# Attention rounds in another order: value products between projection and transposes, parts turned in halves, long products spread over the rounds

## The chip, the cores and the metric

The kernel runs on one core of a Trainium2 chip. The metric is the device time of one launch in microseconds (us), the median over several runs. The page and the trace come from one more launch under the hardware profiler. Engines are TensorE (PE), its weight load (PEld), VectorE (DVE), ScalarE (ACT), GpSimd (POOL) and SyncE (SP), which issues the DMAs.

## The reference

A block of four layers on `x` of 4 x 256 x 512 in fp32, each with a residual and a layer norm ahead of it. Only the first one, attention, is touched:

```python
x = x + _L0_attn_a_ref(_layernorm(x), ...)      # attention with an adapter
x = x + _L0_ffn_ref(_layernorm(x), ...)         # clustered linear layer
x = x + _L0_attn_b_ref(_layernorm(x), ...)      # state-space mixer
x = x + _L0_ffn_ref(_layernorm(x), ...)
```

Attention has 4 batches of 256 tokens, 32 heads of 16 channels, rotary embedding, a causal mask, and a second softmax over 10 adapter rows:

```python
q, k, v = split(x @ w_attn.T);  q, k = rope(q), rope(k)
y = softmax(causal(q @ k.T / sqrt(16))) @ v
y = y + gating * softmax(q @ ak.T / sqrt(512)) @ av
return y @ w_proj.T
```

## The kernel before

`attention` takes the first 370 us or so of the launch, `mixer` the rest. fp32 products against weights are made as three products of fp32r halves (`mm3`, L107 to L114): a "long" product of 128 tokens with a 512 x 512 weight is 12 matmuls of 512 columns.

Attention runs in rounds. Round `i` belongs to batch `b = i // 8` and to four heads, `u = i % 8`; there are 32 rounds and seven more for what trails behind. Each stage of the four heads runs in a round of its own:

- `scores` (L410 to L446), round `i`: 8 products of q and k parts into four `sc` buffers and 4 that add the mask (L427, L434), then on DVE a maximum (`nmx`, L439) and on ACT eight exps (L442).
- `turn` (L448 to L459), one round later: 12 transposes of `e` into three `ptr` buffers, copied to `eT` by DVE (two) and ACT (one).
- `weigh` (L461 to L479), two rounds later: 16 value products into `py`, copied to `ys` by ACT.
- `gathered` (L481 to L492), three rounds later: 2 transposes of `ys` (`try`), then 1/sum and a product on DVE into `y`.

The parts that `scores` reads, for eight heads at a time, are made by `pieces(b, q)`: of q (`f = 0`) and k (`f = 1`) and both token halves, a stack is filled (`stacked`: a cast on ACT, a subtraction on POOL, L304 and L305) and turned by four transposes (`trp`, L379). DVE copies the q parts to `pc0`, ACT the k parts to `pc1` (L381). Each `f` has two stack buffers (`NS = 2`). All 16 transposes stand at the end of every even round, for the next two.

Around these run jobs, Python generators that yield the name of the place in a round at which they go on: "long", "turn" or "values". They are `prepared(b + 1)` (norm, two q, two k and two v products of the next batch; the rotation `rotated` is three DVE products that read `pq`, L280 to L284, and a POOL addition), `adapter` (the adapter's keys and values, once), `adapted(b)` (adapter softmax, `pt` and `pya`), `closed` (adds the adapter's part, turns `y`, and makes the output projection `po`), and `fed` (one tile of 128 tokens of the next layer, `Feed`). `adapter_scores` makes one `pa` product per even round and one `tra` transpose. A job goes on at the next round's place of that name.

PE's instructions are issued exactly in the order of the Python program (`manual_schedule`); the other engines' order is set by the framework. So the order of the calls in a round is PE's order:

```python
es_[i] = scores(b, u)
step("long", i)
... adapter_scores ...
eTs[i - 1] = turn(es_.pop(i - 1))
gathered(*divmod(i - 3, 8), yss.pop(i - 3))
step("turn", i)
step("values", i)
yss[i - 2] = weigh(*divmod(i - 2, 8), eTs.pop(i - 2))
... pieces, in even rounds ...
```

PSUM is split in three pools: three buffers "m" for all products and transposes except scores (`sc`, four buffers) and values (`py`, one). A buffer is taken again when ACT or DVE has read it.

The long products fall as follows: `prepared` in rounds 1, 2, 4, 5, 6, 7 of a batch (for the later batches 9, 10, 12 to 15 and 17, 18, 20 to 23), `po` of batches 0, 1 and 2 as two at once in rounds 12, 20 and 28, `fed` tiles in rounds 29 to 34.

Of the kernel before, what the change touches and what calls it, by code (L numbers as in the profile page):

```python
# [20 lines left out]
P = 128  # L21
# [56 lines left out]
def hybrid_kernel(  # L78
# [153 lines left out]
    def attention(later):  # L232
        with ExitStack() as es:
# [84 lines left out]
            def adapter_weights():  # L318
                pk = ps.tile([80, C], F32, name="pk", tag="m")
                mm3(pk, [[v[:, k, :] for v in wt] for k in range(KC)],  # L320
                    [[v[:, k, :] for v in wk_s] for k in range(KC)])
                ak = p2.tile([80, NH, HD], F32, name="ak", tag="t1")
                bdk = col("bdk")[:20].unsqueeze(1).unsqueeze(3).to_broadcast([20, NH // 2, 2, HD])
                nc.vector.tensor_tensor(
                    ak[:20].rearrange("p (b e) d -> p b e d", e=2),
                    pk[:20].rearrange("p (b e d) -> p b e d", e=2, d=HD), bdk, ALU.mult,
                )
                for q in range(4):
                    s = stacked(ak[:20, q * 8 : q * 8 + 8, :], 1, 20)
# [26 lines left out]
            def prepared(b):  # L356

                where = (ps, "m") if b else (ps_s, "sc")
                xs = []
                for c in range(2):  # L360
                    yield "turn"
                    xs.append(normed(norm, 2 * b + c))
                    for f, w in ((0, wq_s), (1, wk_s)):
                        yield "long"
                        qk[b, c, f] = rotated(projected(xs[c], w, where), c, f, f"r{f}{c}")
                for c in range(2):
                    yield "long"
                    nc.scalar.copy(vs[b % 2][:, c, :C], projected(xs[c], wv_s, where))

            def pieces(b, q):  # L370

                out = []
                for f in range(2):
                    o = p2.tile([P, 4, L], F32R, name=f"pc{f}", tag=f"pc{f}")
                    for c in range(2):
                        s = stacked(qk[b, c, f][:, q * 8 : q * 8 + 8, :], f)
                        tr = ps.tile([P, 4, P], F32R, name="trp", tag="m")
                        for j in range(4):
                            nc.tensor.transpose(tr[:, j, :], s[:, j * P : (j + 1) * P], con)  # L379
                        cs = slice(c * P, (c + 1) * P)  # L380
                        nc.scalar.copy(o[:, :, cs], tr) if f else nc.vector.tensor_copy(o[:, :, cs], tr)  # L381
                    out.append(o)
                turned_[b, q] = out

# [28 lines left out]
            def scores(b, u):  # L413
# [18 lines left out]
                for c, pr, sc in made:  # L432
# [4 lines left out]
                    )  # L437
                    nm = p3.tile([P, 2], F32, name="nmx", tag="nmx", bufs=6)
                    nc.vector.tensor_reduce(nm, sc, AX.X, ALU.max, negate=True)  # L439
# [55 lines left out]
            def adapted(b):  # L495
# [12 lines left out]
                nc.gpsimd.tensor_tensor(sc, sc, wide(sa), ALU.mult)  # L508
                yield "turn"
                paTs = []  # L510
                for c in range(2):
# [7 lines left out]
                    nc.scalar.copy(paTs[c], pt)  # L519
                yield "values"  # L520
                for c in range(2):
# [8 lines left out]
            def closed(b, ks):  # L530

                st = state[b]
                for k in ks:
                    y = st["y"][:, :, k * P : (k + 1) * P]
                    nc.vector.tensor_tensor(y, y, st["ya"][:, :, k * P : (k + 1) * P], ALU.add)
                yield "turn"
                for k in ks:
# [5 lines left out]
                if 3 not in ks:  # L543
                    return
                yield "long"
                st = state.pop(b)
                pos = []
                for c in range(2):
                    pos.append(ps.tile([P, C], F32, name="po", tag="m"))
                    cs = slice(c * P, (c + 1) * P)  # L550
                    mm3(pos[c], [[v[:, k, cs] for v in st["yT"]] for k in range(KC)],
                        [[v[:, k, :] for v in wp_s] for k in range(KC)])
                for c, po in enumerate(pos):
                    t = 2 * b + c
                    ins = nc.vector.tensor_tensor(x[:, t, :], x[:, t, :], po, ALU.add)
                    if t == TT - 1:
                        tc.keep_in_program_order(ins)
                    if feed is None:
                        continue
                    feed.norm.stats(t)  # L560
                    feed.norm.root(t, t + 1)
                    if b < B - 1:
                        slow.append(fed(feed, t))
                    else:
                        late[t] = p2.tile([P, C], F32, name="axn", tag="t1")
                        feed.norm.scale(t, late[t])
                for t, xn in late.items():
# [3 lines left out]
                    late[t] = xs  # L571

            def fed(f, t):
                yield "turn"
                xs = normed(f.norm, t)
                yield "long"
                f.tile(t, xs, [ps.tile([P, FH], F32, name="pd", tag="m") for _ in range(2)])
# [32 lines left out]
            def adapter():  # L610
                split(wt, wte_s)
                yield "long"
                adapter_weights()
                yield "long"
                asides.append(adapter_scores(0, 0))
                next(asides[-1])
                adapter_values()
# [3 lines left out]
            feed, late = None, {}  # L621
            asides, at = [], {}

            def begun(j):
                at[j] = next(j, None)
                if at[j]:
                    jobs.append(j)

            def step(stage, i):

                for j in [j for j in jobs if at[j] == stage and moved.get(j) != i]:
                    moved[j] = i
                    at[j] = next(j, None)
                    if at[j] is None:
                        jobs.remove(j)

            moved = {}
            begin(0)
            pieces(0, 0)
            with tc.manual_schedule(engines={nc.tensor.engine}):  # L640
                for i in range(n + 7):
                    b, u = divmod(i, 8)
                    if i < n:
                        if i == 0:
                            begun(adapter())
                        if u == 0:
                            if i:
                                begin(b)
                            if b + 1 < B:
                                begun(prepared(b + 1))  # L650
                        es_[i] = scores(b, u)
                    if i == n - 6:
                        inner.close()
# [8 lines left out]
                        slow += [fed(feed, t) for t in range(4)]  # L662
                    if slow and i >= n - 4:
                        begun(slow.pop(0))
                    step("long", i)
                    if i < n and u % 2 == 0 and i > 0:
                        asides.append(adapter_scores(b, u // 2))
                        next(asides[-1])
                    if 1 <= i <= n:
                        eTs[i - 1] = turn(es_.pop(i - 1))  # L670
# [572 lines left out]
```

## Time and profile before

| | us |
|---|---|
| median of 3 runs | 1904.89 (1898.11 to 1905.41) |
| profiled execution | 1901.88 |
| its span | 1900.1 |
| attention rounds 0 to 30 | 294.98, PE busy 260.75 |
| one exp of 256 columns, ACT | 0.47 |
| four `nmx`, DVE | 1.95 |
| rotation, three DVE products | 0.69, 0.41, 0.41 |
| `eT`, `pc` copy, DVE / ACT | 0.68 / 0.59 |
| stack cast ACT, subtraction POOL | 0.41, 0.46 |

A row of stretches, as shown below, gives the length, then for each engine its busy time and, in brackets, the number of its instructions. A line of waits names the waiting engine, tile and line, what it waited for, and the total, the number and the longest in us. In a timeline a row is start, duration, engine, line and operation; in brackets the idle time ahead of it and what ended it. PE's ends are modelled, so small overlaps are normal.

### The profile page before, as it was taken

The numbers are of one execution on the slowest core, as the hardware profiler recorded it, in microseconds if no ns is written. First come the engines' busy times: TensorE is split into PE (matmuls) and PEld (weight loads), VectorE is DVE, ScalarE is ACT, GpSimd is POOL, SyncE is SP. The second block draws the span as 40 slices with busy tenths as digits, with TensorE's granted clock in tenths as the row PEclk, the third lists the DMA queues.
The fourth block names the chain that finished last, engine by engine and source line by source line (L and its number), as shares of the span: only waits on it lengthen the run. The fifth ranks groups of instructions, "written<-read, shape, count | busy, mean of one in ns | idle before, by whom it ended". The sixth has DMA issues, their size and how long they took to land.

```text
span 1900.1 us, 29893 instructions
## 1 busy us (share of the span) xinstructions
PE 1817.5 (96%) x10690; PEld 1452.2 (76%) x10690; DVE 1477.0 (78%) x2324; ACT 1381.4 (73%) x2873; POOL 350.2 (18%) x308
## 2 busy tenths in 40 slices
PE   7988889889999999999999999999999999999997
PEld 5766667777777887878788788777787888787786
DVE  5666667778998778777977797778778877877777
ACT  5676686468898767867877787678777876786753
POOL 5221110011221221121212122211211121122100
PEclk8999999989999999999999999999999999999999
DMA  4000000025555544554544454545454544455341
GB/s 142 1 1 1 22 14 1 23 65 172 172 183 183 155 162 147 159 168 148 167 160 156 145 183 139 173 143 171 151 172 141 159 156 165 144 161 166 112 124 49
DMA packets 151909, 240.35 MB, mean 126 GB/s; under 512 B 12368, under 2 KB 77520, under 8 KB 151760
## 3 DMA queue, kind: packets, MB, share of 16 engines
q1 hardware_dynamic: 151760, 238.44, 39.1%
q8 instruction: 84, 1.38, 0.3%
q14 instruction: 65, 0.53, 0.1%
HBM read 202.75 MB, written 35.65 MB: 125 GB/s over the span
## 4 chain that ended last, share of the span: by engine, by line
PE 77%; DVE 9%; ACT 8%; DMA 2%; issue 2%; POOL 1%; SPq 0%; DVEq 0%; ACTq 0%; POOLq 0%
PE pp L112 12%; PE pp L113 12%; PE pp L114 11%; PE pyy L961 8%; PE pog L112 6%; PE pog L114 6%; PE pog L113 6%; PE trx L946 3%; ACT e L442 3%; DVE acc L887 2%; DMA wor<-in_wout_dram 1%; PE ptr L457 1%; PE sc L427 1%; DVE nmx L439 1%; PE py L467 1%
## 5 line engine op out<-in xcount | busy, mean ns | idle before, releaser
L112 PE MATMUL pp<-mx,w 128*128 128x512 f32 (+1 forms) x1160 | 465.4, 401 | 7.9 <-DVE acc L887 7.4
L113 PE MATMUL pp<-mx,w 128*128 128x512 f32 (+1 forms) x1160 | 454.1, 391 | 0.0
L114 PE MATMUL pp<-mx,w 128*128 128x512 f32 (+1 forms) x1160 | 453.8, 391 | 0.0
L887 DVE SCALAR_TENSOR_TENSOR acc<-pp,cw_s,acc 128x1012 f32<-128x1012 f32 (+2 forms) x240 | 304.9, 1270 | 23.2 <-ACT acc L880 22.6
L935 DVE TENSOR_TENSOR em<-em,gm 128x1536 f32<-128x1536 f32 x128 | 228.2, 1783 | 93.9 <-ACT em L929 85.4
L112 PEld LDWEIGHTS pp<-mx,w 128*128 128x128 f32 x1160 | 218.5, 188 | 65.6 <-issue 10.2
L114 PEld LDWEIGHTS pp<-mx,w 128*128 128x128 f32 x1160 | 218.5, 188 | 45.6 <-issue 0.4
L113 PEld LDWEIGHTS pp<-mx,w 128*128 128x128 f32 x1160 | 218.7, 189 | 40.7 <-issue 0.7
L984 POOL TENSOR_TENSOR sq<-sq,acc 128x1024 f32<-128x1024 f32 x55 | 132.6, 2411 | 577.4 <-ACT acc L983 577.4
L923 POOL TENSOR_SCALAR_AFFINE_SELECT r<-r 128x512 f32<-128x512 f32 x128 | 133.7, 1045 | 542.8 <-DMA r<-cumd 441.2
L104 ACT CAST w<-wr 128x512 fp32r<-128x512 f32 x144 | 88.5, 615 | 188.7 <-PE pp L113 165.8
L112 PE MATMUL pog<-wo,gh 128*128 128x512 f32 x512 | 204.6, 400 | 0.0
L928 ACT ACTIVATE em<-r,col_t 128x128 f32<-128x128 f32 x512 | 165.0, 391 | 48.8 <-PE pyy L961 47.0
L113 PE MATMUL pog<-wo,gh 128*128 128x512 f32 x512 | 200.1, 391 | 0.0
L114 PE MATMUL pog<-wo,gh 128*128 128x512 f32 x512 | 199.9, 391 | 0.0
L961 PE MATMUL pyy<-em,xd 128*64 128x256 f32 (+1 forms) x2048 | 189.1, 329 | 3.1 <-DVE em L935 3.1
L961 PEld LDWEIGHTS pyy<-em,xd 128*64 128x64 f32 x2048 | 133.9, 137 | 64.6 <-issue 21.4
L931 ACT ACTIVATE em<-r,col_t 128x128 f32<-128x128 f32 x512 | 166.5, 388 | 0.0
L919 DVE TENSOR_SCALAR em<-r,col_t 128x128 f32<-128x128 f32 x512 | 137.3, 327 | 12.3 <-PE pyy L961 10.1
L947 DVE TENSOR_TENSOR xd<-trx,dt_t 128x512 f32<-128x512 f32 x128 | 86.2, 683 | 54.4 <-PE trx L946 54.3
L105 DVE TENSOR_TENSOR w<-wr,w 128x512 fp32r<-128x512 f32 x139 | 97.9, 705 | 38.1 <-ACT w L104 38.1
L442 ACT ACTIVATE e<-sc,nmx 128x256 f32<-128x256 f32 (+1 forms) x256 | 103.7, 431 | 24.9 <-DVE nmx L439 24.9
(287 smaller groups left out, 3180.4 us busy)
## 6 DMA issues: line engine op xcount, KB each, us to landing
wr<-in_win_dram SPq DMA_DIRECT2D x287, 256.0 KB, 2.8
r<-cumd SPq DMA_DIRECT2D x128, 512.0 KB, 4.1
spill<-gb SPq DMA_DIRECT2D x63, 512.0 KB, 2.8
gr<-spill SPq DMA_DIRECT2D x120, 256.0 KB, 3.4
wor<-in_wout_dram SPq DMA_DIRECT2D x64, 256.0 KB, 3.1
out_dram<-x SPq DMA_DIRECT2D x8, 256.0 KB, 2.3
x<-in_x_dram SPq DMA_DIRECT2D x1, 1536.0 KB, 10.3
gr<-spill SPq DMA_DIRECT2D x8, 192.0 KB, 2.6
```

The lines of the kernel that those rows point to most:

```text
L112: nc.tensor.matmul(o, lh, rh, start=(first and k == 0), stop=False)
L113: nc.tensor.matmul(o, lh, rl, start=False, stop=False)
L114: nc.tensor.matmul(o, ll, rh, start=False, stop=(last and k == n - 1))
L442: nc.scalar.activation(es_[c][:, 2 * j + pr, :], sc[:, j, :], AF.Exp, bias=nm[:, j : j + 1], accum_out=rs[:, c, h : h + 1],)
L887: nc.vector.scalar_tensor_tensor(av[:, :, d:], pv[:, :, : L - d], cw_s[:, ch, tap : tap + 1], av[:, :, d:], ALU.mult, ALU.add,)
L919: nc.vector.tensor_scalar(e[:, b, 2, :], rv[:, b, 1, :], col_t[:, h, b, 1:2], 0.0, ALU.subtract, ALU.min,)
L923: nc.gpsimd.affine_select(rv[:, :, 0, :], rv[:, :, 0, :], pattern=[[0, B], [1, P]], compare_op=ALU.is_ge, fill=-1e30, base=0, channel_mult ...
L928: nc.scalar.activation(e[:, b, 1, :], rv[:, b, 1, :], AF.Exp, bias=col_t[:, h, b, 2:3])
L931: nc.scalar.activation(e[:, b, 0, :], rv[:, b, 0, :], AF.Exp, bias=col_t[:, h, b, 0:1])
L935: nc.vector.tensor_tensor(e, e, gm, ALU.mult)
L961: nc.tensor.matmul(py[d, b, k * P :], xd[:, 2 * b + k, d], es2[hh][:, b, 2 * k : 2 if k == 0 else 3, :].rearrange("p s i -> p (s i)"), sta ...
L984: (nc.gpsimd if n < NB - 1 else nc.vector).tensor_tensor(sq, sq, x2, ALU.add)
```

## The change

Within a round, `weigh` and the "values" place now come after the long products and the parts, and ahead of `turn` and `gathered`. `pieces` is now a generator for one `f`: its first half fills two stacks at the end of a round, its second half turns them in the next round, behind the long product; q parts in even rounds, k parts in odd ones. Jobs yield a place and the earliest round, `FEEDS` names the rounds that start a `Feed` tile, and `begun` and `jobs` become `moved` and `nexts`. `closed` makes its two projections in two rounds (14 and 15, 22 and 23, 28 and 29); only the last batch makes both at once. `prepared` has its long products in rounds 2 to 7, 9 to 14 and 17 to 22. The adapter's keys are made at the "turn" place of round 1, its values and first scores in round 2. `Feed` is opened at round 24 instead of 26. `nmx` has four buffers, not six. The loop has one empty round less.

```diff
+                return ak
+
+            def adapter_keys(ak):
                 for q in range(4):
                     s = stacked(ak[:20, q * 8 : q * 8 + 8, :], 1, 20)
...
                 where = (ps, "m") if b else (ps_s, "sc")
+                r = 8 * (b - 1)
                 xs = []
+
+                def made(c, f):
+                    w = wk_s if f else wq_s
+                    qk[b, c, f] = rotated(projected(xs[c], w, where), c, f, f"r{f}{c}")
+
+                yield "turn", r
+                xs.append(normed(norm, 2 * b))
+                yield "long", r + 1
+                made(0, 0)
+                yield "turn", r + 1
+                xs.append(normed(norm, 2 * b + 1))
+                yield "long", r + 2
+                made(0, 1)
+                yield "long", r + 3
+                made(1, 0)
+                yield "long", r + 4
+                made(1, 1)
                 for c in range(2):
-                    yield "turn"
-                    xs.append(normed(norm, 2 * b + c))
-                    for f, w in ((0, wq_s), (1, wk_s)):
-                        yield "long"
-                        qk[b, c, f] = rotated(projected(xs[c], w, where), c, f, f"r{f}{c}")
+                    yield "long", r + 5 + c
+                    nc.scalar.copy(vs[b % 2][:, c, :C], projected(xs[c], wv_s, where))
+
+            def pieces(b, q, f):
+
+                st = [stacked(qk[b, c, f][:, q * 8 : q * 8 + 8, :], f) for c in range(2)]
+                yield
+                o = p2.tile([P, 4, L], F32R, name=f"pc{f}", tag=f"pc{f}")
                 for c in range(2):
-                    yield "long"
-                    nc.scalar.copy(vs[b % 2][:, c, :C], projected(xs[c], wv_s, where))
-
-            def pieces(b, q):
-
-                out = []
-                for f in range(2):
-                    o = p2.tile([P, 4, L], F32R, name=f"pc{f}", tag=f"pc{f}")
-                    for c in range(2):
-                        s = stacked(qk[b, c, f][:, q * 8 : q * 8 + 8, :], f)
-                        tr = ps.tile([P, 4, P], F32R, name="trp", tag="m")
-                        for j in range(4):
-                            nc.tensor.transpose(tr[:, j, :], s[:, j * P : (j + 1) * P], con)
-                        cs = slice(c * P, (c + 1) * P)
-                        nc.scalar.copy(o[:, :, cs], tr) if f else nc.vector.tensor_copy(o[:, :, cs], tr)
-                    out.append(o)
-                turned_[b, q] = out
+                    tr = ps.tile([P, 4, P], F32R, name="trp", tag="m")
+                    for j in range(4):
+                        nc.tensor.transpose(tr[:, j, :], st[c][:, j * P : (j + 1) * P], con)
+                    cs = slice(c * P, (c + 1) * P)
+                    nc.scalar.copy(o[:, :, cs], tr) if f else nc.vector.tensor_copy(o[:, :, cs], tr)
+                turned_.setdefault((b, q), []).append(o)
+                yield
...
-                    nm = p3.tile([P, 2], F32, name="nmx", tag="nmx", bufs=6)
+                    nm = p3.tile([P, 2], F32, name="nmx", tag="nmx", bufs=4)
...
-                yield "turn"
+                yield "turn", 8 * b + 8
...
-                yield "values"
+                yield "values", 8 * b + 9
...
-                yield "long"
                 st = state.pop(b)
                 pos = []
                 for c in range(2):
+                    if c == 0 or b < B - 1:
+                        yield "long", 8 * b + {B - 1: 0, B - 2: 12}.get(b, 14) + c
                     pos.append(ps.tile([P, C], F32, name="po", tag="m"))
                     cs = slice(c * P, (c + 1) * P)
                     mm3(pos[c], [[v[:, k, cs] for v in st["yT"]] for k in range(KC)],
                         [[v[:, k, :] for v in wp_s] for k in range(KC)])
+                    if b < B - 1:
+                        finished(b, c, pos[c])
+                if b < B - 1:
+                    return
                 for c, po in enumerate(pos):
-                    t = 2 * b + c
-                    ins = nc.vector.tensor_tensor(x[:, t, :], x[:, t, :], po, ALU.add)
-                    if t == TT - 1:
-                        tc.keep_in_program_order(ins)
-                    if feed is None:
-                        continue
-                    feed.norm.stats(t)
-                    feed.norm.root(t, t + 1)
-                    if b < B - 1:
-                        slow.append(fed(feed, t))
-                    else:
-                        late[t] = p2.tile([P, C], F32, name="axn", tag="t1")
-                        feed.norm.scale(t, late[t])
+                    finished(b, c, po)
                 for t, xn in late.items():
                     tr = ps.tile([P, KC, P], F32, name="tr", tag="m")
                     xs = [p2.tile([P, KC, P], F32R, name=f"axs{j}", tag=f"axs{j}") for j in range(2)]
                     feed.norm.turn(xn, tr, xs)
                     late[t] = xs
...
+            def finished(b, c, po):
+                t = 2 * b + c
...
+                feed.norm.stats(t)
+                feed.norm.root(t, t + 1)
+                if b < B - 1:
+                    slow.append(fed(feed, t))
+                else:
+                    late[t] = p2.tile([P, C], F32, name="axn", tag="t1")
+                    feed.norm.scale(t, late[t])
+
             def fed(f, t):
-                yield "turn"
+                yield "turn", 0
                 xs = normed(f.norm, t)
-                yield "long"
+                yield "long", 0
                 f.tile(t, xs, [ps.tile([P, FH], F32, name="pd", tag="m") for _ in range(2)])
...
             def adapter():
                 split(wt, wte_s)
-                yield "long"
-                adapter_weights()
-                yield "long"
+                yield "long", 0
+                ak = adapter_weights()
+                yield "turn", 0
+                adapter_keys(ak)
+                yield "long", 2
                 asides.append(adapter_scores(0, 0))
                 next(asides[-1])
                 adapter_values()
...
+            asides, nexts = [], {}
+            FEEDS = (25, 26, 27, 29, 31, 32)
+
+            def moved(j, i):
+
+                v = next(j, None)
+                if v is None:
+                    nexts.pop(j, None)
+                else:
+                    nexts[j] = v[0], v[1] if v[1] else i + 1
 
             def step(stage, i):
 
-                for j in [j for j in jobs if at[j] == stage and moved.get(j) != i]:
-                    moved[j] = i
-                    at[j] = next(j, None)
-                    if at[j] is None:
-                        jobs.remove(j)
-
-            moved = {}
+                for j in [j for j, (s, r) in nexts.items() if s == stage and r <= i]:
+                    moved(j, i)
...
             begin(0)
-            pieces(0, 0)
+            for f in range(2):
+                for _ in pieces(0, 0, f):
+                    pass
+            part = pieces(0, 1, 0)
+            next(part)
+            moved(adapter(), -1)
             with tc.manual_schedule(engines={nc.tensor.engine}):
-                for i in range(n + 7):
+                for i in range(n + 6):
                     b, u = divmod(i, 8)
                     if i < n:
-                        if i == 0:
-                            begun(adapter())
                         if u == 0:
                             if i:
                                 begin(b)
                             if b + 1 < B:
-                                begun(prepared(b + 1))
+                                moved(prepared(b + 1), i)
                         es_[i] = scores(b, u)
-                    if i == n - 6:
+                    if i == n - 8:
                         inner.close()
                         feed = Feed("f", *(
...
-                    if slow and i >= n - 4:
-                        begun(slow.pop(0))
+                    if i in FEEDS:
+                        moved(slow.pop(0), i - 1)
                     step("long", i)
+                    if part:
+                        next(part)
+                    part = None
                     if i < n and u % 2 == 0 and i > 0:
                         asides.append(adapter_scores(b, u // 2))
                         next(asides[-1])
+                    step("values", i)
+                    if 2 <= i <= n + 1:
+                        yss[i - 2] = weigh(*divmod(i - 2, 8), eTs.pop(i - 2))
                     if 1 <= i <= n:
                         eTs[i - 1] = turn(es_.pop(i - 1))
...
                     if i < n and u == 7:
-                        begun(adapted(b))
-                    step("values", i)
-                    if 2 <= i <= n + 1:
-                        yss[i - 2] = weigh(*divmod(i - 2, 8), eTs.pop(i - 2))
+                        moved(adapted(b), i)
                     if 3 <= i < n + 3:
                         if (i - 3) % 8 == 6:
-                            begun(closed((i - 3) // 8, (0, 1, 2)))
+                            moved(closed((i - 3) // 8, (0, 1, 2)), i)
                         if (i - 3) % 8 == 7:
-                            begun(closed((i - 3) // 8, (3,)))
-                    if i < n and u % 2 == 0:
-                        if u < 6:
-                            pieces(b, u // 2 + 1)
-                        elif b + 1 < B:
-                            pieces(b + 1, 0)
-                assert not jobs and not slow
+                            moved(closed((i - 3) // 8, (3,)), i)
+
+                    b, u = divmod(i + 3, 8)
+                    if b < B and i < n:
+                        part = pieces(b, u // 2, (i + 1) % 2)
+                        next(part)
+                assert not nexts and not slow
```

More of the change, by code (lines that the diff above doesn't have):

```diff
@@ L571, in closed @@
                     late[t] = xs
+            def finished(b, c, po):
+                t = 2 * b + c
+                ins = nc.vector.tensor_tensor(x[:, t, :], x[:, t, :], po, ALU.add)
+                if t == TT - 1:
+                    tc.keep_in_program_order(ins)
+                if feed is None:
+                    return
+                feed.norm.stats(t)
[5 more added lines that the diff above has]
+                    feed.norm.scale(t, late[t])
             def fed(f, t):
-                yield "turn"
+                yield "turn", 0
                 xs = normed(f.norm, t)
-                yield "long"
+                yield "long", 0
                 f.tile(t, xs, [ps.tile([P, FH], F32, name="pd", tag="m") for _ in range(2)])
@@ L611, in adapter @@
                 split(wt, wte_s)
-                yield "long"
-                adapter_weights()
-                yield "long"
+                yield "long", 0
+                ak = adapter_weights()
+                yield "turn", 0
+                adapter_keys(ak)
+                yield "long", 2
                 asides.append(adapter_scores(0, 0))
@@ L621, in attention @@
             feed, late = None, {}
-            asides, at = [], {}
-            def begun(j):
-                at[j] = next(j, None)
-                if at[j]:
-                    jobs.append(j)
-            def step(stage, i):
-                for j in [j for j in jobs if at[j] == stage and moved.get(j) != i]:
-                    moved[j] = i
-                    at[j] = next(j, None)
-                    if at[j] is None:
-                        jobs.remove(j)
-            moved = {}
-            begin(0)
-            pieces(0, 0)
+            asides, nexts = [], {}
[6 more added lines that the diff above has]
+                    nexts[j] = v[0], v[1] if v[1] else i + 1
+            def step(stage, i):
+                for j in [j for j, (s, r) in nexts.items() if s == stage and r <= i]:
+                    moved(j, i)
+            begin(0)
+            for f in range(2):
[4 more added lines that the diff above has]
+            moved(adapter(), -1)
             with tc.manual_schedule(engines={nc.tensor.engine}):
-                for i in range(n + 7):
+                for i in range(n + 6):
                     b, u = divmod(i, 8)
                     if i < n:
-                        if i == 0:
-                            begun(adapter())
                         if u == 0:
```

## The prediction

> **What bounds the kernel now.** I read the page first. TensorE (PE) is busy nearly throughout and the chain that ended last is mostly PE's:
>
> ```profile
> span 1900.1 us, 29893 instructions
> PE 1817.5 (96%) x10690; PEld 1452.2 (76%) x10690; DVE 1477.0 (78%) x2324; ACT 1381.4 (73%) x2873; POOL 350.2 (18%) x308
> ...
> PE 77%; DVE 9%; ACT 8%; DMA 2%; issue 2%; POOL 1%; SPq 0%; DVEq 0%; ACTq 0%; POOLq 0%
> ```
>
> So the number of PE instructions, which the change leaves alone, sets the floor; only PE's idle time in attention, and its clock there, can be won. I cut the trace at the first score product of each attention round, 35.79 to 330.77 us for rounds 0 to 30. The columns are length, then busy time with the instruction count of PE, PEld, DVE, ACT and POOL, then granted clock, DMA share and GB/s:
>
> ```profile
> 129.40:139.89 10.49, 9.76 (x86) 7.79 (x83) 8.68 (x20) 7.05 (x27) 1.72 (x3) 1.00 0.00 1
> 139.89:147.46 7.57, 5.62 (x49) 3.63 (x49) 5.04 (x12) 6.03 (x23) 1.35 (x4) 0.88 0.01 2
> 147.46:163.22 15.76, 15.28 (x104) 12.16 (x100) 9.18 (x19) 6.54 (x25) 2.03 (x3) 0.95 0.00 0
> 163.22:170.39 7.17, 6.51 (x56) 5.00 (x55) 4.94 (x12) 4.58 (x21) 1.88 (x3) 1.00 0.01 2
> ...
> sum 294.98, PE 260.75 PEld 202.57 DVE 189.04 ACT 204.77 POOL 50.67; mean PE 8.41 PEld 6.53 DVE 6.10 ACT 6.61 POOL 1.63
> ```
>
> PE idles 294.98 - 260.75 = 34.2 us in these rounds. Round 11 has no long product: 1.95 us idle and a clock of 0.88; round 12 has three and idles 0.48. The waits of PE in attention say what ends the idle time:
>
> ```profile
> PE try L484 <- DVE eT L458: 6.0, 9, 1.0
> PE ptr L457 <- DVE t L284: 4.0, 6, 0.7
> PE ptr L457 <- DVE eT L458: 3.9, 6, 1.0
> PE try L484 <- ACT av L368: 2.4, 3, 0.8
> ```
>
> Nearly all are waits for one of the three "m" PSUM buffers to be emptied. The timeline of round 9 shows one: after the long product (last issue 123.39) two `ptr` tiles go out, and the third waits for the rotation, which still reads `pq`:
>
> ```profile
> 123.63 1.04 PE L457 MATMUL ptr<-con,e 128*128 128x128 f32 x8
> 125.33 0.63 PE L457 MATMUL ptr<-con,e 128*128 128x128 f32 x4 [0.66 <-DVE t L284]
> ```
>
> Last, shorter stretches of the same table show the clock where transposes stand without a long product:
>
> ```profile
> 143.50:147.00 3.50, 2.55 (x20) 1.29 (x24) 1.88 (x5) 2.77 (x12) 0.00 (x0) 0.80 0.00 0
> 147.00:150.50 3.50, 3.50 (x30) 2.64 (x23) 2.02 (x7) 1.15 (x4) 0.00 (x0) 0.72 0.00 0
> 280.00:290.50 10.50, 9.80 (x64) 7.42 (x64) 6.14 (x14) 7.74 (x32) 0.00 (x0) 0.67 0.01 2
> ```
>
> [...] the dips (0.67 to 0.80) begin in stretches of transposes in rounds 11, 16, 24 and 25. [...] Here `sa` starts at 134.26, just behind the eight exps that end at 134.16. [...]
>
> **The change part by part.** No instruction count changes: 16 part transposes in every second round become 8 in each, the value products keep their 16 matmuls per round, and no DMA or queue entry is added. The Feed's loads on SP's queue are now written two rounds earlier; they already ran in round 24 (DMA share 0.23, 61 GB/s at 266.04 to 276.43), as soon as the value weights, whose space they take, had their last use in round 23. Now that use is in round 22, and nothing else stands in SP's queue then. Their splits on ACT and DVE move with them, one round, and stay beside PE's work.
>
> 1. *Odd rounds with a long product* (5, 7, 9, 13, 15, 17, 21, 23) idle 7.41 us now. New order: scores 0.97, long 2.83, two part tiles 0.93, values 0.95, then `ptr`. The first `ptr` comes 1.9 us after the long product instead of at once, and the rotation takes 1.3 us (0.69 + 2 x 0.41, overlapping) from 0.2 us after it, so that wait goes. Next late is the emptying of the part tiles: for keys, which fall in odd rounds, that is two ACT copies of 0.59 behind the exps, which end 4.98 us after the round's start (round 9): 5.6 and 6.2. PE wants these buffers at about 6.1 and 6.5. That just fits. A `try` then follows three `ptr` in 1.25 us, while the first copy by DVE takes about 1.35 from the start of it: 0.2 stays. I take 0.4 per round, with the two `pya` tiles that 9 and 17 now have ahead of the values: 3.2. **Saves 4.2** (bounds: 6 if nothing waits; -10 if ACT is a copy later).
>
> 2. *Odd rounds that get a long product* (3, 11, 19; 27 a Feed tile) idle 6.22 now: `ptr` waits for exps with nothing in between. With the long product between I take 0.4 each, 0.6 for 27: 1.8. **Saves 4.4** (2 to 5.5).
>
> 3. *Even rounds with a long product, and 26*, idle 9.41 in twelve. Here the query parts stand ahead of the adapter's score tile `pa`: `pq` and two part tiles fill the three buffers, and `pa` waits for the same rotation as `ptr` did, 0.66. The wait is moved, not removed. `sa`'s wait (0.41 in round 10) and the parts' wait for DVE (0.19) go, for the values cover them; `try` and `tra` get about 0.2 each. Seven rounds at 1.05 (2, 4, 6, 10, 12, 18, 20) and five at 0.7 make 10.8. **Costs 1.4** (from +3 to -5).
>
> 4. *Rounds 8, 16, 24, 25, 29* idle 7.04. Three of them keep no long product; eight fewer transposes but the same exps and `pt` tiles: 1.5 each, with 25 at 1.0 and 29 at 0.6: 6.1. **Saves 0.9** (-2 to +3).
>
> 5. *Rounds 0 and 1*, 4.12: the adapter's keys, 16 transposes with waits for POOL (1.73 and 0.72), leave round 0 and go to the end of round 1. Their four stack fills still share two buffers with the key parts. 3.3. **Saves 0.8** (-2 to +2.5).
>
> 6. *Clock.* Lost time is (1 - clock) x length: 0.20 x 3.5 + 0.28 x 3.5 = 1.7 us at 143.5 to 150.5, and 0.33 x 10.5 = 3.5 at 280 to 290.5. Round 11 gets a long product, so the first goes; round 26 gets a Feed tile, but 24 and 25 stay bare, so half the second. The dips of rounds 1, 16 and 24 stay. **Saves 3.4** (0 to 9).
>
> 7. *The end.* The Feed tiles move from rounds 29 to 34 to 26, 27, 28, 30, 32 and 33, PE work that is only moved. The last one (355.40 to 358.7) no longer lies between the values of round 31 and the last `try`: `ys` takes 0.29 + 0.37, PE is bare for about 0.7. But that tile's DVE work no longer delays the last `y` (359.55 in this trace, 0.9 after its `try`), and in round 33 it lies beside `pya` (2.05) and the values. **Saves 1.0** (-2 to +2).
>
> `nmx` with four buffers for six costs nothing: a round makes four, and the exps of the round before have read theirs some 3 us earlier (they end 4.98 us into a round of 7.2, the first reduction starts 0.9 us into the next). If the exps ran late they would hold the four `sc` buffers too, so that wait is there already.
>
> Sum: 4.2 + 4.4 - 1.4 + 0.9 + 0.8 + 3.4 + 1.0 = 13.3 us. The mixer after attention is untouched. Span 1900.1 - 13.3 = 1886.8, and with the 1.8 us around it (1901.9 for the profiled execution) 1888.6. The median 1904.9 is 3.0 above the profiled execution, so 1891.6 by the runs, 0.7% less.
>
> **The rivals.**
>
> - *The wait only changes place.* ACT is at 204.77 of 294.98 us, and in odd rounds part 1 leaves only 0.3 to 0.5 us for it. If the key parts' copies come 0.9 us later than worked, PE loses about 0.6 in each of 14 odd rounds, 8 us: 1900. For it: the chain of waits has ACT `e` at 3% of the span although ACT isn't the busiest. Against it: the exps end well before the copies are wanted.
> - *Nearly all is won.* The values cover every buffer wait: idle time falls to 15 us (19 won), and 5 of the clock's and 1 at the end: 25 us, 1880. For it: values are the only work in a round that needs no "m" buffer besides scores, and they stand now where all buffers are full. Against it: part 3.
> - *Slower.* The stack fills for the next round's parts (two ACT casts 0.41, two POOL subtractions 0.46) are asked for at the end of a round, and PE wants them 3.8 us into the next, 1.0 where no long product stands. Before, all four fills had two rounds. If a fill lands in ACT's FIFO behind the exps, it comes at about 4.98 + 0.82 + 0.6 = 6.4, and PE stands 2.6 us. In a third of 29 rounds that is 25 us, less 13: 1917. It decides from 13.3 / 29 = 0.46 us a round on. Against it: exps wait for the first `nmx`, 1.65 us into a round, and round 8's casts (118.62 to 121.06) fitted ahead of them at 121.48.
>
> **How the numbers follow.** Chances: the forecast (8 to 20 us won) 0.43, nearly all won 0.22, the wait moved 0.23, slower 0.12. The range 1877 to 1903 takes in the bounds of parts 1, 3 and 6 and the first two rivals, and leaves out most of the slower one and a few larger gains. Half a per cent is 9.5 us, about what a measurement of this kernel can tell from no change: the forecast and the second rival are mostly beyond it (0.62), the first within it with the forecast's edge (0.26), the last slower (0.12).
>
> **What would show it.** Right: `ptr` waits on DVE `t` are gone and `pa` waits on DVE `t` have come, about 0.7 in even rounds; no dip of the clock in round 11; the rounds from 0 to 30 idle about 25 us; the last `po` starts within 3 us of the last values. Wrong: `ptr` waiting on ACT `pc` (first rival) or `trp` on POOL `st` (third); no `pa` wait (second); a mixer that differs by more than 3 us.

## The result and the profile after

The changed kernel takes 1901.76 us (median of 12 runs, 1898.68 to 1905.67), the kernel before 1902.21 beside it: a ratio of 1.0002 with a 95% interval of 0.9989 to 1.0014. Timed once more with the experiments it gave 1.0000 (0.9991 to 1.001). The change moves the time by nothing that can be measured; 0.7% less was forecast.

The page of the changed kernel, its first lines:

```profile
span 1897.1 us, 29902 instructions
PE 1813.4 (96%) x10690; PEld 1450.5 (76%) x10690; DVE 1474.0 (78%) x2324; ACT 1381.5 (73%) x2875; POOL 370.0 (20%) x308
```

The number of PE instructions is the same. In this one execution the span is 3.0 us shorter. But the execution took 1898.88 us, 2.9 less than the median of its kernel, so the 3.0 is not a gain of the runs. The table of stretches, cut again at the first score product of each round, has rounds 7, 9, 13, 24, 25 and the sum of rounds 0 to 30:

```profile
101.42:110.37 8.95, 7.26 (x64) 5.69 (x64) 5.54 (x11) 6.59 (x25) 2.77 (x3) 1.00 0.01 2
118.63:130.10 11.47, 10.05 (x85) 7.95 (x84) 7.18 (x16) 7.65 (x26) 2.10 (x3) 1.00 0.01 1
...
157.71:165.09 7.38, 7.25 (x64) 5.71 (x62) 3.18 (x7) 5.95 (x24) 0.23 (x1) 1.00 0.01 2
...
259.31:269.94 10.63, 7.72 (x66) 5.97 (x66) 8.79 (x20) 8.54 (x28) 3.85 (x5) 0.84 0.00 0
269.94:280.32 10.38, 7.59 (x71) 6.18 (x70) 4.07 (x9) 9.04 (x28) 0.87 (x2) 0.92 0.01 2
...
sum 295.06, PE 262.68 PEld 206.28 DVE 194.00 ACT 206.70 POOL 50.67; mean PE 8.47 PEld 6.65 DVE 6.26 ACT 6.67 POOL 1.63
```

PE's idle time in these rounds is 32.4 us; it was 34.2, and about 25 was forecast. Round 13 shows what was hoped for (0.13 us idle), rounds 7 and 9 (1.7 and 1.4) what came instead. Rounds 24 and 25, which are bare (they have no long product), idle 2.9 and 2.8. The waits of PE, 36 to 375 us, name the new ones:

```profile
PE ptr L471 <- ACT pc L395: 5.6, 5, 2.8
PE pa L403 <- DVE t L284: 5.5, 6, 1.0
PE pd L112 <- ACT axs L104: 4.4, 3, 2.9
PE ptr L471 <- DVE pc L395: 3.4, 3, 2.4
```

The waits of `ptr` on the rotation are gone. `pa` waits for it in six even rounds, as forecast. `ptr` now waits for the copies of the part tiles, mostly the k parts' on ACT, and a Feed tile for its normed input. The timeline of round 9 shows the first kind (the last of eight exps, the two k copies, the next PE work that needs a buffer):

```profile
123.52 0.40 ACT L456 ACTIVATE e<-sc,nmx 128x128 f32<-128x128 f32 x1
...
123.86 1.11 ACT L395 CAST pc<-trp 128x512 fp32r<-128x512 f32 x2
...
124.53 2.05 PE L538 MATMUL pya<-avbd,paT 80*128 80x128 f32 x16 [1.19 <-ACT pc L395]
```

The copies were ready to start at about 123.0, when the first part tile was done, and stood behind the exps until 123.86. In round 7 the exps themselves are late. The adapter's exp stands ahead of them and waits for POOL; the last of the eight starts at 107.54, 6.1 us into the round (in round 9 it is 4.9), and only then comes the copy of the v product (`av`) that `ptr` waits for:

```profile
104.07 0.74 ACT L517 ACTIVATE as<-as 128x640 f32<-128x640 f32 x1 [2.26 <-POOL as L516]
...
107.54 0.40 ACT L456 ACTIVATE e<-sc,nmx 128x128 f32<-128x128 f32 x1
...
108.55 1.63 PE L471 MATMUL ptr<-con,e 128*128 128x128 f32 x12 [1.69 <-ACT av L383]
```

The timeline of PE in rounds 31 and 32 shows the other kind:

```profile
336.06 0.66 PE L163 MATMUL tr<-con,axn 128*128 128x128 f32 x4 [0.16 <-DVE eT L472]
339.59 0.40 PE L112 MATMUL pd<-fw,axs 128*128 128x288 f32 x1 [2.87 <-ACT axs L104]
340.72 0.44 PE L112 MATMUL pd<-fw,axs 128*128 128x288 f32 x1
```

Round 31 has no long product. PE runs ahead through it, to the transposes of the next Feed tile, whose copy on ACT (338.89) stands behind the adapter's exp, the round's eight exps and two more copies. PE stands idle for 2.87 us, and the granted clock in the 3.9 us after that is 0.56. Two stretches, before and after 339.6 us:

```profile
336.50:339.60 3.10, 0.23 (x4) 0.01 (x1) 1.71 (x7) 3.04 (x13) 1.39 (x3) 1.00 0.00 0
339.60:343.50 3.90, 3.70 (x15) 3.47 (x16) 1.01 (x3) 0.00 (x0) 0.01 (x1) 0.56 0.00 0
```

### The profile page after: what moved, and what is told of

Read it like the earlier page. It is cut to its first block, busy times and chain, and to the rows that moved or that the text cites. A ratio compares the mean times of both kernels' runs of the same rounds, so it can differ in the third digit from the quotient of the medians.

```text
span 1897.1 us, 29902 instructions
## 1 busy us (share of the span) xinstructions
PE 1813.4 (96%) x10690; PEld 1450.5 (76%) x10690; DVE 1474.0 (78%) x2324; ACT 1381.5 (73%) x2875; POOL 370.0 (20%) x308
## 4 chain that ended last, share of the span: by engine, by line
PE 75%; DVE 9%; ACT 9%; DMA 3%; issue 3%; POOL 1%; SPq 0%; DVEq 0%; ACTq 0%; POOLq 0%
PE pp L112 12%; PE pp L113 11%; PE pp L114 11%; PE pyy L991 8%; PE pog L112 6%; PE pog L114 6%; PE pog L113 6%; PE trx L976 3%; ACT e L456 3%; PE ptr L471 2%; DMA wor<-in_wout_dram 2%; DVE acc L917 1%; PE pd L114 1%; ACT L921 1%; DVE eT L472 1%
## 5 line engine op out<-in xcount | busy, mean ns | idle before, releaser
L953 POOL TENSOR_SCALAR_AFFINE_SELECT r<-r 128x512 f32<-128x512 f32 x128 | 153.0, 1196 | 526.7 <-DMA r<-cumd 433.8
```

The lines of the kernel that those rows point to most:

```text
L953: nc.gpsimd.affine_select(rv[:, :, 0, :], rv[:, :, 0, :], pattern=[[0, B], [1, P]], compare_op=ALU.is_ge, fill=-1e30, base=0, channel_mult ...
```

## The experiments

All ratios are against the kernel before, with 95% intervals of 0.1 to 0.2% to either side. All but two (7 and 10) are edits of the changed kernel.

**1. The k parts' copies on DVE.**

```diff
-                    nc.scalar.copy(o[:, :, cs], tr) if f else nc.vector.tensor_copy(o[:, :, cs], tr)
+                    nc.vector.tensor_copy(o[:, :, cs], tr)
```

> The changed kernel, with the k parts' PSUM tiles copied by DVE instead of ACT. Theory (the gain went into new waits for particular late copies): the waits of ptr and pya on ACT pc (5.6 and 2.4 us in the changed kernel's trace) go, rounds 9, 17 and 25 idle about 1 us less each; DVE has 0.69 x 28 = 19 us more work in 300, mostly beside PE's long products: 4 to 7 us faster than the changed kernel, about 1896. Rival (three buffers and the work of ACT and DVE behind them set the idle time, whichever copy is late): the waits come back on DVE pc and eT, within 2 us of the changed kernel.

1897.15 us, ratio 0.9969 (0.9959 to 0.9979): 0.31% faster, 6 us, inside the theory's 4 to 7. The sum of rounds 0 to 30 and the row of round 13:

```profile
156.48:163.67 7.19, 7.19 (x64) 5.74 (x63) 4.47 (x9) 5.18 (x22) 0.92 (x2) 1.00 0.01 2
...
sum 290.99, PE 262.98 PEld 204.46 DVE 209.84 ACT 192.38 POOL 49.63; mean PE 8.48 PEld 6.60 DVE 6.77 ACT 6.21 POOL 1.60
```

Idle time is 28.0 us, 4.4 less. DVE took 16 us more work and ACT 14 less. About half of the waits was handed on: those of `ptr` and `pya` on ACT `pc` (5.6 and 2.4 us) are gone, those of `ptr` on DVE `pc` grew from 3.4 to 5.4 us, and `pya` waits 2.5 us for DVE. The eight odd rounds of the forecast's first step (5, 7, 9, 13, 15, 17, 21, 23) idle 3.55 us instead of 7.02. Rounds 9 and 17 gained only 0.3 each where 1 us was expected, because `pya` then waits for the rotation (0.9); round 25 gained 1.2.

**2. A Feed tile in round 31.**

```diff
-            FEEDS = (25, 26, 27, 29, 31, 32)
+            FEEDS = (25, 26, 27, 29, 30, 32)
```

> The changed kernel, with one Feed tile a round earlier (its long product in round 31 instead of 32), so that round 31 isn't bare. Theory: PE's wait of 2.9 us for the normed tile at 336.7 to 339.6 us and the half clock after it (0.57 over 3.5 us, 1.5 us) go: 3 to 4 us faster than the changed kernel. Round 32 has then no long product, but its exps are done, so about 0.5 to 1 of it comes back. Rival (the end of attention is a chain from the last exps to the mixer that no tile's place changes): within 1 us.

1898.13 us, ratio 0.9978 (0.9967 to 0.9988): 0.22%, 4 us. PE's timeline in its rounds 31 and 32 (the tile's first matmul, then `ptr` and the first values of round 32):

```profile
332.26 0.38 PE L112 MATMUL pd<-fw,axs 128*128 128x288 f32 x1
...
338.40 0.63 PE L471 MATMUL ptr<-con,e 128*128 128x128 f32 x4 [0.65 <-DVE fx L216]
...
340.69 0.64 PE L481 MATMUL py<-eT,av 128*32 128x256 f32 x8 [1.17 <-DVE eT L472]
```

The idle 2.87 us and the clock of 0.56 are gone (1.00 from round 31 to the last `po`); 1.8 us of other waits came in their place. The last `po` ends at 361.23 us, with the changed kernel at 365.33.

**3. `pa` behind the values.** The block of `adapter_scores` moves below `weigh`.

```diff
-                    if i < n and u % 2 == 0 and i > 0:
-                        asides.append(adapter_scores(b, u // 2))
-                        next(asides[-1])
                     step("values", i)
                     if 2 <= i <= n + 1:
                         yss[i - 2] = weigh(*divmod(i - 2, 8), eTs.pop(i - 2))
+                    if i < n and u % 2 == 0 and i > 0:
+                        asides.append(adapter_scores(b, u // 2))
+                        next(asides[-1])
```

> The changed kernel, with the adapter's score product pa behind the value products instead of ahead of them. Theory: the six waits of pa on the rotation (5.5 us in all) go, since the values' 0.95 us cover the rotation's rest; what comes instead is the third ptr behind the copy of pa on ACT, at most 0.3 a round: 3 to 5 us faster than the changed kernel. Rival: the wait moves whole to ptr, within 1 us.

1897.81 us, ratio 0.9975 (0.9966 to 0.9984): 0.25%, 5 us. Of the 5.5 us that `pa` waited for the rotation 0.2 is left; the twelve even rounds of the forecast's third step idle 6.1 us instead of 11.0. Round 10, first of the changed kernel, then here:

```profile
130.10:140.19 10.09, 9.02 (x76) 6.95 (x76) 7.75 (x17) 6.55 (x25) 2.12 (x3) 1.00 0.00 0
131.69:141.00 9.31, 9.04 (x75) 7.01 (x74) 7.81 (x16) 6.37 (x25) 2.11 (x3) 1.00 0.00 0
```

Its trace is no shorter than the changed kernel's: in that one execution the clock lost 6.9 us more (see the last section).

**4. The three together.** k on DVE, a tile in round 31, `pa` behind the values.

> The changed kernel with the three edits of before together: k copies on DVE, a Feed tile in round 31, pa behind the values. Theory (separate waits at separate places): the gains add, 0.31 + 0.22 + 0.25 = 0.78%, less a little because DVE now also has the k copies in front of pa's turn: 0.55 to 0.8% faster than before, about 1890. Rival (the same idle time is only moved): no better than the best alone, 0.3%.

1889.68 us, ratio 0.992 (0.9908 to 0.9933). The gains add: 0.31 + 0.22 + 0.25 = 0.78, measured 0.80%. Its sum of rounds 0 to 30:

```profile
sum 286.74, PE 264.54 PEld 206.12 DVE 210.78 ACT 192.09 POOL 49.57; mean PE 8.53 PEld 6.65 DVE 6.80 ACT 6.20 POOL 1.60
```

22.2 us idle. The rival, that idle time only moves from one copy to another and no more than 0.3% can be had, falls.

**5. Feed tiles in rounds 25, 26, 27.**

```diff
-            FEEDS = (25, 26, 27, 29, 31, 32)
+            FEEDS = (24, 25, 26, 29, 31, 32)
```

> The changed kernel with the first three Feed tiles a round earlier (long products in rounds 25, 26, 27), so that round 25 isn't bare. Theory (bare rounds): round 25 now idles 2.79 us, waiting at ptr for the k copies behind the exps; with 3.3 us of products in between 0.8 is left, and round 28 idles as much as now: 2 us faster than the changed kernel, 0.1%. Rival (ACT's and DVE's preparation of Feed in round 24 delays them wherever the tile is): within 0.5 us.

1899.1 us, ratio 0.9982 (0.9974 to 0.9991): 0.18%, 3.4 us where 2 were expected. Round 25 idles 0.98 us instead of 2.79. Round 24 idles as before (3.1). In the changed kernel's trace `ptr` waits 2.4 us there for part copies on DVE, which come behind two of the Feed's weight splits (`fw`) and the maxima (`nmx`) that these delay:

```profile
259.78 2.52 DVE L105 TENSOR_TENSOR fw<-fr,fw 128x576 fp32r<-128x576 f32 x2
262.23 1.94 DVE L453 TENSOR_REDUCE nmx<-sc 128x2 f32<-128x512 f32 x4
264.18 1.25 DVE L395 CAST pc<-trp 128x512 fp32r<-128x512 f32 x2
```

A tile can't be moved ahead of its own weights. Most of round 25's gain is lost again in round 29, which idles 1.57 us instead of 0.16, so that all 31 rounds idle 31.8 us against 32.4. Where the runs' 3.4 us come from, this trace doesn't show.

**6. Four edits together.** Experiment 4 with `FEEDS = (24, 25, 26, 29, 30, 32)`.

> The changed kernel with k copies on DVE, pa behind the values, and Feed tiles in rounds 25, 26, 27, 30, 31 and 33. Theory: round 25's idle 1.6 us, which k on DVE left, halves: 0.8 to 0.9% faster than before, about 1887 to 1890. Rival: nothing beyond the three edits' 0.80%, or less, since rounds 28 and 29 have po alone.

1886.52 us, ratio 0.9923 (0.9904 to 0.9942). With the three edits it was 0.992, in another comparison: the intervals don't tell them apart, so the fourth edit is unproven on top. Either is faster than both kernels by about 0.8%.

**7. Values alone.** An edit of the kernel before: only `weigh` and the "values" place move up, behind the adapter's scores.

> The kernel before, with only the value products and the adapter's value products moved up behind the long product and the adapter's scores, ahead of turn; parts still all at the end of even rounds, long products as before. Theory (values there cover the rotation): the waits of ptr on DVE t (4.0 us) and of ptr and try on ACT av (4.5 us) go, in part back as try on eT, 4 to 6 us faster than before, about 1897, because the new waits of the changed kernel come from the parts' place and the bare rounds. Rival (the reorder itself is worth nothing): within 1.5 us of before.

1896.71 us, ratio 0.9968 (0.9956 to 0.9981): 0.32%, 6 us, the upper end of the theory. Its sum of rounds 0 to 30:

```profile
sum 283.73, PE 258.79 PEld 199.46 DVE 189.07 ACT 202.57 POOL 51.12; mean PE 8.35 PEld 6.43 DVE 6.10 ACT 6.53 POOL 1.65
```

24.9 us idle instead of 34.2, with one of three parts of the change.

**8. Parts undone.** The changed kernel with all 16 part transposes at the end of even rounds.

> The changed kernel with the parts as before: all 16 transposes at the end of even rounds, values and long products as changed. Theory A (the halves behind the long product fill the three buffers and cost what the values save): odd rounds lose their waits on ACT pc, pa no longer waits for the rotation: 5 to 7 us faster than the changed kernel, like values alone or better, 0.3 to 0.4% under before. Theory B (the spread of the long products with its bare rounds 24, 25 and 31 costs it): within 2 us of the changed kernel.

1895.93 us, ratio 0.9955 (0.9941 to 0.9969): 0.45%, some 8 us, where the changed kernel gives none. Theory A holds, with a little more than its 5 to 7 us; theory B, within 2 us, falls. 24.2 us idle:

```profile
sum 288.98, PE 264.76 PEld 206.45 DVE 193.82 ACT 207.43 POOL 50.92; mean PE 8.54 PEld 6.66 DVE 6.25 ACT 6.69 POOL 1.64
```

**9. Parts undone, and a tile in round 31.** Experiments 8 and 2 together.

> The changed kernel with the parts at the end of even rounds as before, and with a Feed tile in round 31. Theory: the 4 us that the tile in round 31 gave add to the parts' 0.45%: 0.6 to 0.7% faster than before. Rival (the parts' place only decides which of the end's waits is seen): no better than 0.5%.

1889.94 us, ratio 0.9941 (0.9922 to 0.996): 0.59%, just under the theory; the interval (0.40 to 0.78) leaves room for the rival's 0.5 too. But with the spread and the tile in round 31 the halves cost: 0.22% with them (experiment 2), 0.59% without, and these intervals don't meet.

**10. Spread undone.** The kernel before with values moved up and parts in halves, long products and Feed tiles as before.

> The kernel before with values moved up and the parts in halves, long products and Feed tiles as before. Theory A (the halves cost it): the 6 us that values alone gave are gone, within 2 us of before. Theory B (the spread costs it): still 0.25 to 0.35% faster than before.

1896.35 us, ratio 0.9962 (0.995 to 0.9974): 0.38%. Theory A, that the halves undo what the values give, is refuted here, and theory B's number came: time is as good as with values alone, although its 31 rounds idle 32.7 us. Experiment 8 had refuted theory B. So neither the halves nor the spread takes the gain alone; it goes when they come together.

In idle time the halves cost the same both ways: 24.9 us without and 32.7 with them where the products are as before (7 and 10), 24.2 and 32.4 where they are spread (8 and the changed kernel). Only with the spread did this cost the runs time. In this trace the clock loses 6.8 us less than before, by (1 - clock) x length, and the execution was the fastest of its six, 2.7 us under the median. The kernel keeps the Feed tiles in rounds 29 to 34, so that round 31 isn't bare; experiment 2 recovers 0.22% of the 0.38 by that alone. What the rest is, the runs leave open.

**11. Values undone.** The changed kernel with `weigh` and "values" back at the end of the round.

> The changed kernel with the value products back at the end of the round. Theory (values behind the parts are what covers the rotation and the part copies): ptr then follows the parts and pa directly, with all three buffers full: some 0.8 to 1.3 us more idle in each of 28 rounds, partly bare already: 15 to 25 us slower than the changed kernel, 0.8 to 1.3% over before. Rival (their place is worth the same 6 us as in the kernel before): 0.3% over before.

1901.8 us, ratio 0.9992 (0.9984 to 1.0001). Theory and rival both fall: no slower than the changed kernel. The rounds do idle 6 us more, 300.07 - 261.37 = 38.7 against 32.4:

```profile
sum 300.07, PE 261.37 PEld 205.12 DVE 195.09 ACT 208.41 POOL 50.39; mean PE 8.43 PEld 6.62 DVE 6.29 ACT 6.72 POOL 1.63
```

But from the first score product of round 31 to the last `po` it takes 30.6 us against 33.9, and in this trace the clock doesn't dip between 60 and 366 us. So the same move that gave 0.32% in the kernel before gives nothing beside the halves and the spread. Whether the shorter end and the better clock belong to the order, one trace doesn't show.

**12. The changed kernel again.**

> The changed kernel as it is, timed once more beside the others. Theory (its gain and its new waits cancel): 0.0 to -0.25% against before; its trace ended attention 2.6 us earlier, 0.14%. Rival (the first comparison was an odd one and the change does gain like its parts, values with halves 0.38%, values with the spread 0.45%): -0.3% or better.

1902.82 us, ratio 1.0000 (0.9991 to 1.001). The whole gives nothing, which is the theory's upper end, though values with halves give 0.38% and values with the spread 0.45%. Its trace has nearly the idle time of the first one in rounds 0 to 30, 296.83 - 263.49 = 33.3 us:

```profile
sum 296.83, PE 263.49 PEld 206.20 DVE 194.32 ACT 206.82 POOL 50.66; mean PE 8.50 PEld 6.65 DVE 6.27 ACT 6.67 POOL 1.63
```

## Why the prediction was wrong

The mechanism was half right: the waits of `ptr` on the rotation went, but copies that were worked as being in time came late in three of the seven steps. Step by step, in PE's idle time of the same classes of rounds (step 6: (1 - clock) x length in stretches of 3.5 us up to the last `po`), minus for a gain. The second trace is that of experiment 12, the same kernel:

| step of the prediction | forecast, us | trace, us | second trace, us |
|---|---|---|---|
| 1 odd rounds with a long product | -4.2 | -0.4 | -0.2 |
| 2 odd rounds that get one | -4.4 | -4.3 | -4.2 |
| 3 even rounds | +1.4 | +1.5 | +1.5 |
| 4 rounds 8, 16, 24, 25, 29 | -0.9 | +1.3 | +1.8 |
| 5 rounds 0 and 1 | -0.8 | 0.0 | +0.2 |
| 6 clock | -3.4 | -3.5 | -1.7 |
| 7 the end (PE idle from round 31 to the last `po`: 3.97 before, then 6.18 and 6.01) | -1.0 | +2.2 | +2.0 |
| sum | -13.3 | -3.2 | -0.6 |

- **Step 1 failed**: "That just fits." It does in rounds 5, 13 and 21 (0.13 or 0.14 idle). In rounds 7, 15 and 23 the adapter's exp (0.74) stands in ACT's queue ahead of the eight exps and itself waits for POOL, so that they end about 6.6 us into the round; the working took round 9's 4.98 for every round. In 9 and 17 `pya` wants a buffer right behind the parts, 4.7 us into the round, where the working had PE ask at 6.1; the tiles were counted as work but not as a demand for buffers. This is the first rival, "the wait only changes place", in kind. Its total, 1900, is nearest to the result, but by luck: it put 8 us on the odd rounds, and here they lack 3.8. Experiment 1 takes the copies off ACT and gets near the step's sum (3.55 idle; 3.2 forecast), though not as 0.4 in each round: rounds 7, 9 and 17 keep about 1.1, the other five 0.1 or less.
- **Step 7 failed** because the places of the tiles were listed (26, 27, 28, 30, 32, 33) and the hole at 31 not read from them: round 31 is the last with exps and also has the adapter's exp. Experiment 2 gives 4 us back for one number.
- **Step 4 failed** because it took round 24 for a round like 8 and 16, and 25 for a lighter one at 1.0; of the four rounds without a long product it named three. It left out the table switches on ACT (two of 1.28 us) and the Feed's weight splits on DVE (2.52 us ahead of round 24's maxima), which the prediction had left "beside PE's work". Experiment 5 recovers round 25, at the price of round 29.
- **Step 3 was right** to 0.2 us, and so was **step 2**. The `pa` wait was forecast and left as a cost; experiment 3 shows that most of it could be had for a move of three lines.
- **Step 5** was a small miss: the waits of the adapter's keys for their stack fills on POOL cost 3.1 us in round 1, where they cost 2.5 in round 0.
- **Step 6** agrees in size by chance: in the first trace 5.2 us came in rounds 0 to 30 and 1.7 went at round 32, and the second trace of the same kernel has half of it. That a long product takes a dip away was the author's estimate from the profile before; what sets a dip off, no run shows.
- The rival of late stack fills did not come: `trp` never waits for POOL in the changed kernel.

What stays open is why the halves cost the runs nothing without the spread (experiment 10) and the values give nothing with both (experiment 11).

## What to carry to other kernels

Work that needs no buffer of a shared pool can be worth moving to where that pool is full (0.32% in the kernel before). Ask then what empties the tiles that are put ahead of it, and behind what in that engine's queue: taking two copies from behind eight exps gave 6 us, where the whole change was to give 13. Work out such a queue for each kind of round, not for one. When long products are spread, list the rounds that stay bare and look at each one's queues, above all the last ones. Three small waits at separate places added up to their sum when mended, 0.80%.

## What the runs showed of the hardware that was not expected

The dips of PE's clock don't fall in the same places in two executions of the same instructions. The changed kernel's two profiles, 1897.1 and 1901.6 us long, in the same stretches; first one, then the other:

```profile
199.50:206.50 7.00, 6.76 (x64) 5.38 (x64) 3.93 (x10) 3.26 (x7) 1.24 (x3) 1.00 0.00 0
262.50:269.50 7.00, 4.14 (x21) 3.30 (x22) 5.60 (x15) 5.91 (x21) 1.36 (x4) 0.76 0.00 0
...
339.50:346.50 7.00, 6.71 (x48) 5.95 (x49) 3.36 (x11) 0.81 (x4) 0.10 (x3) 0.76 0.00 0
```

```profile
199.50:206.50 7.00, 6.67 (x52) 5.06 (x52) 2.81 (x7) 3.05 (x7) 1.60 (x3) 0.76 0.00 0
262.50:269.50 7.00, 4.17 (x42) 2.73 (x40) 6.53 (x13) 5.65 (x21) 3.29 (x5) 1.00 0.00 0
...
339.50:346.50 7.00, 5.09 (x20) 4.87 (x21) 2.17 (x9) 2.26 (x9) 1.39 (x3) 0.58 0.00 0
```

What a dip costs depends on what it falls on. Rounds 17 and 24, first of the one profile, then of the other:

```profile
193.10:204.56 11.46, 10.03 (x83) 7.92 (x82) 7.17 (x16) 7.66 (x26) 2.10 (x3) 1.00 0.00 0
259.31:269.94 10.63, 7.72 (x66) 5.97 (x66) 8.79 (x20) 8.54 (x28) 3.85 (x5) 0.84 0.00 0
```

```profile
193.47:206.49 13.02, 11.50 (x83) 8.92 (x82) 7.26 (x16) 7.67 (x26) 2.10 (x3) 0.87 0.00 0
261.23:271.44 10.21, 6.76 (x66) 4.82 (x66) 8.82 (x20) 8.72 (x28) 3.85 (x5) 1.00 0.00 0
```

By (1 - clock) x length each dip is worth 1.7 us. In round 17, which has a long product, it made the round 1.6 us longer. In round 24, where `ptr` waits 2.4 us for DVE in the first profile, it made it 0.4 us longer. A bare round doesn't always bring a dip: round 16 is bare in all three profiles, at 0.85 before and 1.00 in both of the changed kernel.

The mixer, which no edit touches, varies too: from the last `po` to the end of the span it took 1529.6 us (experiment 10) to 1535.7 (experiment 8) in the traces. Experiment 3 spread over 12.5 us in 22 runs (1891.07 to 1903.57). So the span of a single trace of this kernel can't show a gain of 3 us. Against the kernel before, the end of the last `po` came closer: in the thirteen traces it was 1.2 us off the runs' gain on average (at most 3.0), the span 2.0 (at most 4.1).
